# Two graph layers on one core: a head that shares the third pass's banks, moments on GpSimd, and a split weight load

## The chip, the cores and the metric

The kernel runs on one core of one Trainium2 chip. The metric is device time in microseconds (us) of one execution, lower being better; a kernel's time is the median of several executions. The engines are named as the profile names them: PE (matrix products), DVE (vector), ACT (scalar), POOL (GpSimd) and SP, which here only issues DMAs. PEld is PE's loading of stationary operands.

## The reference

Sixteen graphs of 1024 nodes with 128 channels go through two layers. Each layer ends in a residual sum and a normalisation over the channels. Cut to what matters:

```python
h = x                                              # layer 0: gated, 4 steps
for i in range(4):
    m = einsum('bjn,bjd->bnd', adj, h @ weight[i])
    gx, gh = m @ w_ih[i].T + b_ih[i], h @ w_hh[i].T + b_hh[i]
    r, z = sigmoid(xr + hr), sigmoid(xz + hz)      # thirds of gx and gh
    n = tanh(xn + r * hn)
    h = (1 - z) * n + z * h
x = layernorm(x + h * mask)

adj_d = dilate(adj)                                # layer 1: row by row, sequential
for k in 1, 2, 3:
    out = (adj_d @ h / deg) @ Wr[k] + h @ Wx[k] + b[k]
    h = h_k = bn(relu(out / norm(out) * mask))     # bn: moments over all graphs and nodes
x = layernorm(x + (concat(h_1, h_2, h_3) @ Wl + bl) * mask)
```

The batch norm of pass 3 takes its moments over all sixteen graphs, so the last product with `Wl` can't be finished for any graph before the third pass has ended for all.

## The kernel before, in words

**Layer 0** is the class `Gated` (`load_weights` L945, `prepare` L966, `load_test` L991, `layer` L1074, `run` L1131). Two streams of graphs alternate, a layer of one and then a layer of the other. A layer multiplies the state, split into two parts (`h_hi`, `h_lo`), with the adjacency matrix (PE, L1092), copies the product (ACT, L1095) and forms the gates from products with `h_wi` and `h_wh` (PE, L1104; DVE L1116 and L1118; ACT L1119; POOL L1123 to L1125). Before the first layer, `load_weights` loads for each of four steps one 128x128 matrix `h_w` and two gate matrices of 384x128 (`w_ih`, `w_hh`), and then two biases, all by ACT's DMA queue. `prepare` turns each of them on PE (L974 for the gates, L977 for `h_w`), evicts them (DVE and ACT, L975 and L978), and folds `h_w` into the first gate matrix (L981, L982). Adjacency (`h_a` L1016, `f_a` L687) and node data (`h_x` L1021) come by POOL's queue, which casts. For a check that the adjacency matrix is binary, `load_test` loads 32 blocks of 128x1024 `h_test` by SP's queue, the first at the start; DVE looks at each (`look`, L2028).

Beside layer 0 runs the dilation, class `FixPoint`: DVE scans (L737) and small operations, wide ACT passes `f_u`, DVE `f_nr` (L866), stores by SP (L867). The two are interleaved by hand: `beside` gives `layer` the work of the other stream and the next step of the dilation at numbered places. Nearly the whole kernel stands in manual schedules, where each engine executes its instructions in the order of the program text; only the stretches outside (`weights`, `head_weights`) are ordered by a planner, which may move an instruction ahead of its place.

**Layer 1** is the class `Sage`: three passes and a head. The **third pass** (`third`, L1875) takes 32 units, two halves of 512 nodes for each graph, in a software pipeline. In iteration i, PE forms the two products of unit i (`out_next`: L1800 into `q_oa`, L1803 and L1806 into `q_ob`) and turns the rows of unit i-3 (`turned`, L1450, into `s_tr`). DVE makes the reciprocal norms of unit i-2 (L1434 to L1436), and POOL scales its rows by them (`rows_by_pool`, L1439, four instructions, into `s_r`); then DVE takes the statistics of unit i-5 over its turned rows `s_r3` (L1909). ACT scales unit i (L1393, into `s_o`), DVE adds to it (L1396), ACT copies the turned rows of unit i-4 (L1916), ACT and DVE share the sums of squares (L1412, L1415, root L1419), and DVE adds the unit's share of the final product to `s_acc` (L1927). `s_o` and `s_r` have three buffers each, the PSUM tiles two. A flag for the binary check is read in iteration 16. Five iterations drain the pipeline; in these the rows are scaled by DVE (L1429).

`head_weights` (L1369) then forms the batch norm from all statistics, scales the last third of `Wl` by it, and makes the constant row `v` by four small products (L1377 and L1380), which `parts` cuts into three bf16 parts (L1343 and following).

The **head** (`last`, L1931) takes sixteen graphs. For each half PE forms four products of 128x128 with the kept rows (L1953), for the second half adds `s_acc` by a product with the unit matrix (L1957, 128x512), and adds the constant row by four short bf16 products with a node mask (L1961, its row `u_rb` from POOL, L1942). DVE adds `s_acc` in the first half (L1964). Then DVE takes statistics (L1968, eight of 128x128 for each graph) and aggregates them to mean and variance (L1970, eight of 128x2). ACT takes the root (L1972), DVE the reciprocal (L1977) and the shift (L1978). The eight blocks are normalised one graph later, one by POOL (L1984), seven by ACT (L1988), and stored by SP (L1990). The head has a pool of eight PSUM banks, two for each graph.

Of the kernel before, what the change touches and what calls it, by code (L numbers as in the profile page):

```python
# [917 lines left out]
class Gated:  # L918
# [28 lines left out]
    def load_weights(self):  # L947
# [262 lines left out]
class Sage:  # L1210
# [664 lines left out]
    def third(self):  # L1875

        nc, tc = self.nc, self.tc
        with ExitStack() as c:
            pool = lambda name, **k: c.enter_context(tc.tile_pool(name=name, **k))
            self.wk = pool("t_wk", bufs=3)  # L1880
            self.ps2 = pool("t_ps2", bufs=2, space=PSUM)
# [7 lines left out]
            for i in range(len(units) + 5):  # L1889
# [17 lines left out]
                if i >= 5:  # L1907
                    b3, f3 = units[i - 5]
                    nc.vector.bn_stats(self.stats[2][:, 2 * b3 + f3, :], self.r3[:, b3, f3, :])  # L1909
# [14 lines left out]
                if i < len(units):  # L1924
                    g["ss", f] = self.shared_squares(g["o", f])
                    acc = self.acc[:, b, 4 * f:4 * f + 4, :]
                    nc.vector.tensor_add(acc, pb[:, :, 1, :], acc)  # L1927


    def last(self, r48):  # L1930
        nc, tc, cst = self.nc, self.tc, self.cst  # L1931
        with ExitStack() as c:
            pool = lambda name, **k: c.enter_context(tc.tile_pool(name=name, **k))
            wk = pool("u_wk", bufs=6)
            ps = pool("u_ps", bufs=8, space=PSUM)
            c.enter_context(tc.manual_schedule(engines={ET.PE, ET.DVE, ET.Activation, ET.Pool, ET.SP}))
            st = {}

            def row(b):
# [4 lines left out]
            def head(b):  # L1944
                rb = st.pop(("row", b))
                row(b + 2)
                y = wk.tile([P, NB, C], F32, name="u_y")
                mv = self.small.tile([P, NB, 2], F32, name="p_mv")
                for f in range(2):
                    acc = self.acc[:, b, 4 * f:4 * f + 4, :]  # L1950
                    pp = ps.tile([P, 4, C], F32, name="u_p")
                    for i in range(4):
                        nc.tensor.matmul(pp[:, i, :], self.r3[:, b, f, i * P:(i + 1) * P], self.wr2,  # L1953
                                         start=(i == 0), stop=False)
                    if f:

                        nc.tensor.matmul(pp.rearrange("p a b -> p (a b)"), cst["ident"],  # L1957
                                         acc.rearrange("p a b -> p (a b)"), start=False, stop=False)
                    for i in range(4):
                        k = 4 * f + i  # L1960
                        nc.tensor.matmul(pp[:, i, :], self.mask48[:, k * P:(k + 1) * P], rb,  # L1961
# [155 lines left out]
```

## Time and profile before

| | |
|---|---|
| median of 3 runs | 2175.93 us (2174.55 to 2177.75) |
| the profiled execution | 2176.16 us |
| its span in the profile | 2174.3 us |
| mean TensorE clock granted | 0.988 of full |
| third pass, first L1800 to last statistics | 1985.86 to 2102.25 us |
| last product of the head ends | 2161.27 us |
| last store issued | 2166.43 us |

One execution was taken by the profiler, and its times are counted from the start of its span. A row of a timeline gives start, duration, engine, line, operation, tiles out<-in, shapes and how many instructions in one row; in square brackets stands how long the engine had been idle before it and what released it. In a table by stage each engine has its busy time and its instructions, followed by the granted clock, the DMA share and the GB/s. In a list of waits, the numbers are us in total, times, and the longest. Matmul ends are modelled. A wait for several events is put down to the one that came last by the profile.

### The profile page before, as it was taken

Reading aid. Unit: us, or ns where it says so; the run is one execution under the profiler, and the core shown is the slowest. Engines: PE = TensorE matmul, PEld = TensorE weight load, DVE = VectorE, ACT = ScalarE, POOL = GpSimd, SP = SyncE. Lnnn points to the kernel's source line nnn. Section 1 sums busy time; section 2 is a strip of 40 time slices with the busy share of each in tenths; the row PEclk is TensorE's granted clock in tenths of the full one; section 3 lists DMA queues with packets and bytes.
Section 4 is the critical chain, followed back from the end, with each engine's and each line's share of the span. In section 5 each row is a group of like instructions: output and inputs, shape, how many; then the busy total and the mean of one; then the engine's idle time right before and its main releaser. Section 6 shows DMA issues by size and latency. Waiting matters only on the chain. (4 is left out here: it accounts for less than half of the span.)

```text
span 2174.3 us, 33161 instructions
## 1 busy us (share of the span) xinstructions
PE 2063.3 (95%) x10217; PEld 1438.1 (66%) x10217; DVE 1831.1 (84%) x4313; ACT 1312.8 (60%) x3142; POOL 1324.3 (61%) x1346
## 2 busy tenths in 40 slices
PE   6999999999999999999999978999999889999987
PEld 3666556666556665566655656777777768887876
DVE  4898998988998889998889978888888777676888
ACT  3657557566565656656566466666666545555757
POOL 4458558567467476476575456777777545555852
PEclk9999999999999999999999989999999999999989
DMA  8348356347446276455394349888888677775515
GB/s 258 77 93 252 92 126 225 82 133 214 101 143 195 75 210 155 96 190 132 79 266 104 74 166 318 305 297 307 304 305 306 209 243 271 265 262 185 158 40 157
DMA packets 233856, 406.16 MB, mean 187 GB/s; under 512 B 79042, under 2 KB 100196, under 8 KB 233668
## 3 DMA queue, kind: packets, MB, share of 16 engines
q1 hardware_dynamic: 187844, 284.37, 40.7%
q0 software_dynamic: 41472, 117.46, 20.1%
q10 hardware_dynamic: 4352, 2.11, 0.4%
q8 instruction: 83, 1.36, 0.3%
q14 instruction: 105, 0.86, 0.1%
HBM read 313.48 MB, written 109.25 MB: 194 GB/s over the span
## 5 line engine op out<-in xcount | busy, mean ns | idle before, releaser
L1104 PE MATMUL h_g<-h_h,h_wh 128*128 128x512 f32 x768 | 396.1, 597 | 3.3 <-DVE h_r L1116 3.3
L1104 PE MATMUL h_g<-h_ms,h_wi 128*128 128x512 f32 x768 | 392.3, 592 | 0.0
L1123 POOL TENSOR_TENSOR h_zh<-h_r,h_h 128x512 f32<-128x512 f32 x126 | 174.1, 1382 | 257.9 <-ACT h_r L1119 254.7
L737 DVE TENSOR_TENSOR_SCAN f_rank<-f_a,f_first,f_pd 128x1024 f16<-128x1024 bf16 x128 | 299.4, 2345 | 4.2
L1092 PE MATMUL h_g<-h_a,h_hi 128*128 128x512 f32 x1024 | 278.6, 413 | 1.1 <-DMA h_a<-in_adj_dram 1.0
L1536 POOL CAST p_b<-p_at 128x512 uint8<-128x512 f32 x256 | 219.4, 878 | 84.3 <-DVE p_at L1528 52.3
L1104 PEld LDWEIGHTS h_g<-h_ms,h_wi 128*128 128x128 f32 x768 | 145.6, 190 | 184.2 <-issue 168.6
L1092 PE MATMUL h_g<-h_a,h_lo 128*128 128x512 f32 x1024 | 261.9, 393 | 0.4 <-DVE h_lo L1030 0.4
L1092 PEld LDWEIGHTS h_g<-h_a,h_hi 128*128 128x128 f32 x1024 | 190.1, 188 | 61.7 <-issue 21.0
L1092 PEld LDWEIGHTS h_g<-h_a,h_lo 128*128 128x128 f32 x1024 | 189.8, 188 | 39.0 <-DVE h_lo L1030 0.8
L1104 PEld LDWEIGHTS h_g<-h_h,h_wh 128*128 128x128 f32 x768 | 133.4, 190 | 100.3 <-issue 72.9
L1125 POOL TENSOR_TENSOR h_h<-h_h,h_zh 128x512 f32<-128x512 f32 x126 | 179.9, 1427 | 9.9
L1119 ACT ACTIVATE h_r<-h_r,h_bi 128x512 f32<-128x512 f32 x128 | 92.4, 722 | 150.1 <-DVE h_r L1118 150.1
L1124 POOL TENSOR_TENSOR h_zh<-h_z,h_zh 128x512 f32<-128x512 f32 x126 | 162.0, 1285 | 9.9
L1095 ACT COPY h_ms<-h_g 128x512 f32<-128x512 f32 x128 | 73.8, 576 | 150.7 <-PE h_g L1092 150.7
L1403 ACT ACTIVATE s_junk<-s_o 128x128 bf16<-128x128 f32 x256 | 76.1, 298 | 141.6 <-DVE s_o L1396 141.6
L910 ACT ACTIVATE f_u<-f_rank,f_q 128x128 f16<-128x128 f16 (+7 forms) x128 | 110.6, 867 | 69.7 <-DVE f_rank L850 69.7
L2028 DVE SCALAR_TENSOR_TENSOR p_junk<-p_a 128x1024 bf16<-128x1024 f32 x96 | 125.8, 1311 | 0.0
L1803 PE MATMUL q_ob<-s_wxp,q_xt 128*128 128x256 f32 x512 | 123.5, 385 | 0.0
L778 POOL TENSOR_SCALAR_AFFINE_SELECT f_both<-f_both 128x512 bf16<-128x512 bf16 x32 | 20.4, 639 | 164.2 <-DVE f_both L777 164.2
L1528 DVE SCALAR_TENSOR_TENSOR p_at<-p_nr,p_u 128x128 fp32r<-128x128 bf16 (+1 forms) x192 | 102.4, 543 | 20.2 <-ACT p_at L1520 14.8
L887 ACT ACTIVATE f_pd<-f_rank,f_q 128x128 f32<-128x128 f16 x128 | 59.1, 462 | 96.6 <-DVE f_q L701 93.4
(273 smaller groups left out, 4900.9 us busy)
## 6 DMA issues: line engine op xcount, KB each, us to landing
h_a<-in_adj_dram POOLq DMA_DIRECT2D x128, 512.0 KB, 9.1
p_a<-in_adj_dram SPq DMA_DIRECT2D x96, 512.0 KB
f_a<-in_adj_dram POOLq DMA_DIRECT2D x128, 256.0 KB, 6.5
e_nr<-f_nr SPq DMA_DIRECT2D x128, 256.0 KB
p_nr<-e_nr SPq DMA_DIRECT2D x32, 1024.0 KB
h_test<-in_adj_dram SPq DMA_DIRECT2D x32, 512.0 KB
s_at<-p_b SPq DMA_DIRECT2D x32, 512.0 KB
s_ag<-s_ag SPq DMA_DIRECT2D x64, 256.0 KB
```

The lines of the kernel that those rows point to most:

```text
L737: nc.vector.tensor_tensor_scan(out, a, other[:, 0, 0:1].to_broadcast([P, N]), start, op0=ALU.add, op1=ALU.bypass)
L910: nc.scalar.activation(u[:, :n1], rank[:, g, :n1], AF.Abs, bias=q[:, 1, g:g + 1], scale=q[:, 0, g:g + 1])
L1092: nc.tensor.matmul(pm[f], part[:, j, :], st.adj[j][:, half[f]], start=(j == 0 and n == 0), stop=(j == NB - 1 and n == 1))
L1104: nc.tensor.matmul(pg, lhs, rhs, start=(i == 0), stop=(i == len(mm) - 1))
L1119: nc.scalar.activation(r, r, AF.Tanh, bias=bias(self.bi, 2))
L1123: aid.tensor_tensor(d, r, h, ALU.subtract)
L1124: aid.tensor_tensor(d, z, d, ALU.mult)
L1125: aid.tensor_tensor(h, h, d, ALU.add)
L1528: self.nc.vector.scalar_tensor_tensor(g["at"][:, j, c0:c0 + low], v[:, j, c0:c0 + low], 0.0, pu[:, :low], op0=ALU.is_lt, op1=ALU.is_lt)
L1536: self.nc.gpsimd.tensor_copy(g["b", f][:, j, :], g["at"][:, j, f * HF:(f + 1) * HF].bitcast(F32))
L1803: nc.tensor.matmul(pb[:, i], g["xt"][:, f, blk], self.wxp, start=(i % 2 == 0), stop=False)
L2028: nc.vector.scalar_tensor_tensor(junk, a, 0.0, a, op0=ALU.is_gt, op1=ALU.not_equal, accum_out=bad[:, c:c + 1])
```

## The change

1. Of the weights of layer 0, the four matrices `w_hh` and both biases are loaded by SP's queue; `h_w` and `w_ih` stay on ACT's.
2. The first `h_test` is loaded by POOL's queue; it stands where the program text has it, after the first layer's work on that queue. The other 31 stay on SP's.
3. In the third pass the statistics (L1909 before) are taken of unit i-4 and stand at the end of the iteration, behind L1927; before they were of unit i-5 and stood behind L1436. The drain has four iterations in place of five. The last L1927 is put off into `head_weights`.
4. Third pass and head share one PSUM pool (`q_oa`, `q_ob`, `s_tr`, two buffers each, eight banks in all), and `head_weights` stands inside the head's manual schedule. A graph whose number leaves 1 or 2 when divided by 4 takes one two-bank tile `q_ob`; the others take two tiles of one bank.
5. In the drain and between the weight products stand the unit-matrix products of the first three graphs (`start_half`) and eight bf16 products of 128x512 whose result nobody reads.
6. In the head, `half` (products with the kept rows) runs two halves ahead of `finish` (the constant row and the statistics).
7. For all graphs but the last, mean and variance come from six POOL instructions on 128x8 (`moments`) in place of eight L1970 on DVE; the factors that this leaves out go into ACT's root and DVE's shift. The last graph keeps the eight L1970.
8. POOL normalises two blocks of each graph in place of one, ACT six in place of seven. The root of graph b follows the normalisation of graph b-1 on ACT. `u_rb` has four buffers in place of three, and DVE makes the first.

```diff
-                nc.scalar.dma_start(t, src[l].rearrange("(g p) c -> p g c", p=C))
+                (nc.scalar, nc.sync)[n].dma_start(t, src[l].rearrange("(g p) c -> p g c", p=C))
         for t, src in zip(self.b_in, (b_ih, b_hh)):
-            nc.scalar.dma_start(t, src.rearrange("l (g c) -> (l g) c", c=C))
+            nc.sync.dma_start(t, src.rearrange("l (g c) -> (l g) c", c=C))
...
-            self.nc.sync.dma_start(self.test, self.adj[n // 2, n % 2 * P:(n % 2 + 1) * P, :])
+            (self.nc.sync if n else self.nc.gpsimd).dma_start(self.test, self.adj[n // 2, n % 2 * P:(n % 2 + 1) * P, :])
...
-    def head_weights(self, ps):
+    def head_weights(self):
         nc, K = self.nc, 3 * B
+        v = self.ps2.tile([P, 4, P], F32, name="s_tr")[:K, 0, :]
+        junk = self.ps2.tile([P, 4, P], F32, name="s_tr").rearrange("p a b -> p (a b)")
         self.batch_norm(2)
         self.scaled(self.wr2, self.wl[:, 2, :], 2)
-        v = ps.tile([K, C], F32, name="s_v48")
         for l in range(3):
             beta = self.small.tile([C, K], F32, name="s_beta48")
             nc.vector.tensor_copy(beta, self.ab[l][:, 1:2].to_broadcast([C, K]))
+            if l == 2:
+                self.start_half(1)
+                for i in range(8):
+                    nc.tensor.matmul(junk, self.cst["ident_b"], self.mask48[:, :HF], start=True, stop=True)
             nc.tensor.matmul(v, beta, self.wl[:, l, :], start=(l == 0), stop=False)
         beta = self.small.tile([C, K], F32, name="s_beta48")
         nc.vector.tensor_copy(beta[:10, :], self.cst["ident"][:10, 9:10].to_broadcast([10, K]))
         nc.tensor.matmul(v, beta[:10, :], self.vr, start=False, stop=True)
+        nc.vector.tensor_add(*self.late)
+        self.start_half(2)
         r48 = self.one.tile([P, C], BF, name="s_r48")
         nc.gpsimd.memset(r48, 0.0)
         self.parts(v, self.part48, r48[:K, :])
         return r48
+
+    def head_banks(self, b):
+        ps = self.ps2
+        if b % 4 in (0, 3):
+            self.banks[b] = [ps.tile([P, 4, C], F32, name="s_tr" if b % 4 else "q_oa") for f in range(2)]
+        else:
+            t = ps.tile([P, 4, 2, C], F32, name="q_ob").rearrange("p a b c -> p (a b) c")
+            self.banks[b] = [t[:, :4, :], t[:, 4:, :]]
+
+    def start_half(self, b):
+
+        acc = self.acc[:, b, 4:, :]
+        self.head_banks(b)
+        self.nc.tensor.matmul(self.banks[b][1].rearrange("p a b -> p (a b)"), self.cst["ident"],
+                              acc.rearrange("p a b -> p (a b)"), start=True, stop=False)
...
-            self.ps2 = pool("t_ps2", bufs=2, space=PSUM)
+            self.banks = {}
...
-            for i in range(len(units) + 5):
+            for i in range(len(units) + 4):
...
+                if i == len(units):
+                    self.start_half(0)
                 if 2 <= i < len(units) + 2:
                     b1, f1 = units[i - 2]
                     g = self.g[b1]
                     rows = self.rows_by_pool if i < len(units) else self.rows
                     g["r", f1] = rows(b1, f1, g.pop(("o", f1)), g.pop(("ss", f1)))
-                if i >= 5:
-                    b3, f3 = units[i - 5]
-                    nc.vector.bn_stats(self.stats[2][:, 2 * b3 + f3, :], self.r3[:, b3, f3, :])
...
-                    nc.vector.tensor_add(acc, pb[:, :, 1, :], acc)
-
-
-    def last(self, r48):
+                    self.late = acc, pb[:, :, 1, :], acc
+                    if i + 1 < len(units):
+                        nc.vector.tensor_add(*self.late)
+                if i >= 4:
+                    b4, f4 = units[i - 4]
+                    nc.vector.bn_stats(self.stats[2][:, 2 * b4 + f4, :], self.r3[:, b4, f4, :])
...
+    def last(self):
         nc, tc, cst = self.nc, self.tc, self.cst
         with ExitStack() as c:
             pool = lambda name, **k: c.enter_context(tc.tile_pool(name=name, **k))
             wk = pool("u_wk", bufs=6)
-            ps = pool("u_ps", bufs=8, space=PSUM)
             c.enter_context(tc.manual_schedule(engines={ET.PE, ET.DVE, ET.Activation, ET.Pool, ET.SP}))
+            r48 = self.head_weights()
             st = {}
             def row(b):
                 if b < B:
-                    st["row", b] = wk.tile([P, C], BF, name="u_rb", bufs=3)
-                    nc.gpsimd.tensor_scalar(st["row", b], r48, self.graph[:, b:b + 1], None, op0=ALU.mult)
...
+                    st["row", b] = wk.tile([P, C], BF, name="u_rb", bufs=4)
+                    (nc.gpsimd if b else nc.vector).tensor_scalar(st["row", b], r48, self.graph[:, b:b + 1], None,
+                                                                  op0=ALU.mult)
+            def half(b, f):
+                ahead = b < 3 and f
+                if f == 0:
+                    row(b + 2)
+                    if b not in self.banks:
+                        self.head_banks(b)
+                pp, acc = self.banks[b][f], self.acc[:, b, 4 * f:4 * f + 4, :]
+                for i in range(4):
+                    nc.tensor.matmul(pp[:, i, :], self.r3[:, b, f, i * P:(i + 1) * P], self.wr2,
+                                     start=(i == 0 and not ahead), stop=False)
+                if f and not ahead:
+                    nc.tensor.matmul(pp.rearrange("p a b -> p (a b)"), cst["ident"],
+                                     acc.rearrange("p a b -> p (a b)"), start=False, stop=False)
+            def finish(b, f):
+                pp, acc = self.banks[b][f], self.acc[:, b, 4 * f:4 * f + 4, :]
+                for i in range(4):
+                    k = 4 * f + i
+                    nc.tensor.matmul(pp[:, i, :], self.mask48[:, k * P:(k + 1) * P], st["row", b],
+                                     start=False, stop=(i == 3))
+                if not f:
+                    st["y", b] = wk.tile([P, NB, C], F32, name="u_y")
+                    st["s6", b] = self.small.tile([P, NB, 6], F32, name="u_st")
+                    nc.vector.tensor_add(st["y", b][:, :4, :], pp, acc)
+                s6, src = st["s6", b], pp if f else st["y", b]
+                for i in range(4):
+                    nc.vector.bn_stats(s6[:, 4 * f + i, :], src[:, i, :])
+            def moments(b):
+                y, pp, s6 = st.pop(("y", b)), self.banks.pop(b)[1], st.pop(("s6", b))
+                st.pop(("row", b))
+                if b < B - 1:
+                    mv = self.small.tile([P, 4, NB], F32, name="u_mv")
+                    total, gap, spread, var = (mv[:, i, :] for i in range(4))
+                    nc.gpsimd.tensor_tensor(gap, s6[:, :, 1], s6[:, :, 4], ALU.subtract)
+                    nc.gpsimd.tensor_tensor(spread, s6[:, :, 2], s6[:, :, 5], ALU.add)
+                    nc.gpsimd.tensor_tensor(gap, gap, gap, ALU.mult)
+                    nc.gpsimd.tensor_scalar(gap, gap, C / 4.0, 0.0, op0=ALU.mult, op1=ALU.add)
+                    nc.gpsimd.tensor_tensor(var, gap, spread, ALU.add)
+                    nc.gpsimd.tensor_tensor(total, s6[:, :, 1], s6[:, :, 4], ALU.add)
+                    st[b] = y, pp, total, var, -0.5, 1.0 / C
+                else:
+                    mv = self.small.tile([P, NB, 2], F32, name="p_mv")
+                    for k in range(NB):
+                        nc.vector.bn_aggr(mv[:, k, :], s6[:, k, :])
+                    st[b] = y, pp, mv[:, :, 0], mv[:, :, 1], -1.0, 1.0
+            def root(b):
+                rs = st["rs", b] = self.small.tile([P, 2, NB], F32, name="u_rs")
+                nc.scalar.activation(rs[:, 0, :], st[b][3], AF.Sqrt, bias=self.eps, scale=st[b][5])
             def norm(b):
...
+                y, pp, mean, _, share, _ = st.pop(b)
+                rs = st.pop(("rs", b))
                 nc.vector.reciprocal(rs[:, 0, :], rs[:, 0, :])
-                nc.vector.scalar_tensor_tensor(rs[:, 1, :], mv[:, :, 0], -1.0, rs[:, 0, :],
+                nc.vector.scalar_tensor_tensor(rs[:, 1, :], mean, share, rs[:, 0, :],
                                                op0=ALU.mult, op1=ALU.mult)
                 for k in range(NB):
                     src = pp[:, k - 4, :] if k > 3 else y[:, k, :]
                     scale, shift = rs[:, 0, k:k + 1], rs[:, 1, k:k + 1]
-                    if k == 0 or (b, k) == (B - 1, 1):
+                    if k < 2:
                         nc.gpsimd.tensor_scalar(y[:, k, :], src, scale, shift, op0=ALU.mult, op1=ALU.add)
                     elif b == B - 1 and k > 2:
                         nc.vector.tensor_scalar(y[:, k, :], src, scale, shift, op0=ALU.mult, op1=ALU.add)
...
             row(0)
             row(1)
...
+            halves = [(b, f) for b in range(B) for f in range(2)]
+            for h in range(len(halves) + 2):
+                if h < len(halves):
+                    half(*halves[h])
+                if h < 2:
+                    continue
+                b, f = halves[h - 2]
+                finish(b, f)
+                if f:
+                    moments(b)
+                    if b == B - 1:
+                        root(b)
+                    if b:
+                        norm(b - 1)
+                    if b < B - 1:
+                        root(b)
+            norm(B - 1)
...
-        self.third()
-        with tc.tile_pool(name="s_psw", bufs=1, space=PSUM) as ps:
-            r48 = self.head_weights(ps)
-        self.last(r48)
+        with tc.tile_pool(name="t_ps2", bufs=2, space=PSUM) as self.ps2:
+            self.third()
+            self.last()
```

More of the change, by code (lines that the diff above doesn't have):

```diff
@@ L1940, in row @@
                 if b < B:
-                    st["row", b] = wk.tile([P, C], BF, name="u_rb", bufs=3)
-                    nc.gpsimd.tensor_scalar(st["row", b], r48, self.graph[:, b:b + 1], None, op0=ALU.mult)
[L1944 to L1961, printed above, removed]
-                                         start=False, stop=(i == 3))
-                    if not f:
-                        nc.vector.tensor_add(y[:, :4, :], pp, acc)
-                    s6 = self.small.tile([P, 4, 6], F32, name="p_st")
-                    src = pp if f else y
-                    for i in range(4):
-                        nc.vector.bn_stats(s6[:, i, :], src[:, i, :])
-                    for i in range(4):
-                        nc.vector.bn_aggr(mv[:, 4 * f + i, :], s6[:, i, :])
-                rs = self.small.tile([P, 2, NB], F32, name="u_rs")
-                nc.scalar.activation(rs[:, 0, :], mv[:, :, 1], AF.Sqrt, bias=self.eps)
-                st[b] = y, pp, mv, rs
@@ L1975, in norm @@
+            def root(b):
+                rs = st["rs", b] = self.small.tile([P, 2, NB], F32, name="u_rs")
+                nc.scalar.activation(rs[:, 0, :], st[b][3], AF.Sqrt, bias=self.eps, scale=st[b][5])
             def norm(b):
-                y, pp, mv, rs = st.pop(b)
+                y, pp, mean, _, share, _ = st.pop(b)
+                rs = st.pop(("rs", b))
                 nc.vector.reciprocal(rs[:, 0, :], rs[:, 0, :])
-                nc.vector.scalar_tensor_tensor(rs[:, 1, :], mv[:, :, 0], -1.0, rs[:, 0, :],
+                nc.vector.scalar_tensor_tensor(rs[:, 1, :], mean, share, rs[:, 0, :],
@@ L1996, in last @@
             row(1)
-            for b in range(B + 1):
-                if b < B:
-                    head(b)
-                if b:
-                    norm(b - 1)
+            halves = [(b, f) for b in range(B) for f in range(2)]
[15 more added lines that the diff above has]
+            norm(B - 1)
     def run(self):
```

## The prediction

> **What bounds the kernel now.** I read the page first, then the waits of the first 45 us, then a table of busy time by stage, then the timelines of the third pass and of the head.
>
> ```profile
> span 2174.3 us, 33161 instructions
> PE 2063.3 (95%) x10217; PEld 1438.1 (66%) x10217; DVE 1831.1 (84%) x4313; ACT 1312.8 (60%) x3142; POOL 1324.3 (61%) x1346
> ```
>
> PE is the bound on average, but the change touches the three places where it is not, or shares the bound. In the start PE waits for weights:
>
> ```profile
> ACT L1056 <- DMA h_z<-in_L_gnn_w_ih_dram: 23.5, 1, 23.5
> PE h_g L974 <- DMA h_r<-in_L_gnn_w_ih_dram: 5.4, 1, 5.4
> PE h_g L974 <- DMA h_z<-in_L_gnn_w_ih_dram: 4.8, 1, 4.8
> PE h_g L974 <- DMA h_r<-in_L_gnn_w_hh_dram: 3.5, 1, 3.5
> PE h_g L974 <- DMA h_z<-in_L_gnn_w_hh_dram: 2.7, 1, 2.7
> ```
>
> ACT's first work comes at 23.5 because its queue is blocked by its own issues (6.54, 4.21 and 4.28 us at three of them). The last weights are turned at 28.02 and the first L1092 starts at 33.81.
>
> In the third pass one loop runs through three engines:
>
> ```profile
> 2072.88 0.68 DVE L1927 TENSOR_TENSOR s_acc<-q_ob,s_acc 128x512 f32<-128x512 f32 x1
> ...
> 2073.48 0.16 DVE L1434 TENSOR_SCALAR s_ss<-s_ss 128x4 f32<-128x4 f32 x1
> ...
> 2073.88 0.17 DVE L1436 TENSOR_TENSOR s_ss<-s_ss,mask 128x4 f32<-128x4 f32 x1
> 2073.97 0.69 DVE L1909 BATCH_NORM_STATS2 s_st<-s_r 128x6 f32<-128x512 f32 x1
> ...
> 2074.24 5.88 POOL L1439 TENSOR_SCALAR s_r<-s_o,s_ss 128x128 f32<-128x128 f32 x8 [0.79 <-PE s_tr L1450]
> ...
> 2077.16 1.14 ACT L1393 ACTIVATE s_o<-q_oa,s_rdeg 128x128 f32<-128x128 f32 x4 [0.70 <-POOL s_r L1439]
> ...
> 2078.39 0.69 DVE L1396 TENSOR_TENSOR s_o<-q_ob,s_o 128x512 f32<-128x512 f32 x1 [0.75 <-ACT s_o L1393]
> ```
>
> Read it as a ring: L1434 to L1436 end at 2074.05, POOL starts 0.19 later, ACT waits for POOL's fourth row, DVE waits for ACT, and L1927 ends where the next L1434 starts. The page names PE as POOL's releaser, but in three successive pairs POOL starts 0.19, 0.19 and 0.18 after L1436 ends and 0.50, 0.60 and 0.69 after L1450 starts: the constant one is the cause. A pair of units takes 6.69; PE needs 3.29 a unit (6.58 a pair), so ring and PE are nearly level.
>
> ```profile
> 2094.00:2107.00 13.00, 5.63 (x23) 2.96 (x22) 10.67 (x33) 4.62 (x15) 2.89 (x4) 0.71 0.00 1
> 2107.00:2114.00 7.00, 6.81 (x33) 5.32 (x34) 3.41 (x17) 0.00 (x0) 2.18 (x4) 0.57 0.00 0
> 2120.00:2156.00 36.00, 36.00 (x297) 29.59 (x297) 35.25 (x215) 32.24 (x91) 11.21 (x22) 1.00 0.58 162
> ```
>
> In the drain PE idles 7.4 us and works at half clock until 2113.0; in the head it is busy 36.00 of 36 (3.20 us a graph), with DVE at 35.25.
>
> ```profile
> 2142.27 0.89 DVE L1968 BATCH_NORM_STATS2 p_st<-u_p 128x6 f32<-128x128 f32 x4
> ...
> 2143.55 0.17 DVE L1978 SCALAR_TENSOR_TENSOR u_rs<-p_mv,u_rs 128x8 f32<-128x8 f32 x1
> ...
> 2143.76 1.26 ACT L1988 ACTIVATE u_y<-u_y,u_rs 128x128 f32<-128x128 f32 x3
> ...
> 2144.92 1.48 ACT L1988 ACTIVATE u_y<-u_p,u_rs 128x128 f32<-128x128 f32 x4
> ```
>
> **What the Trainium skill says.** "DMA: Bandwidth & Descriptors", Queues, rings and completion order: a DMA engine alternates between its queue rows packet by packet. Agrees: from 6 to 26 us POOL's queue moves about 84 packets a us (2 or 4 KB, 173 ns) and ACT's about 89 (512 B, 39 ns). "TensorE: Matmul & The Clock Gate", Part 1: the clock halves after an idle window and needs some 3.4 us of work to return; Part 4: transposes do not count as work. Agrees: last product 2094.1, half clock at 2099.7 though L1450 ran, full at 2113.0. "SBUF — State Buffer", Who interferes with whom: a DVE instruction with one SBUF input does not block GpSimd. So moving L1909 should leave POOL's row at 733 ns; no trace here isolates it. "GPSIMD Engine Reference", 3.1: some 2.6 cycles an element for two inputs, which for 8 elements is under 20 ns as an estimate, so fixed cost rules the new small operations; none is in this trace.
>
> **Part by part.**
>
> 1. *Half the gated weights by SP.* 1536 of 3584 packets leave ACT's row. With three rows a turn takes 173+39+39 = 251 ns instead of 212, so each small row moves 89 x 212/251 = 75 a us. h_test's 128 packets of 4 KB also leave the first 5 us: 128 x 173/16 = 1.4 us in which, at the 540 a us that 512 B packets reach alone, some 750 weights move. At 6 us 739 had landed; now about 1500. Of the other 2084 half per row: 1042/75 = 13.9, so the last lands near 20 by rate, and I take 21.7 (20.5 to 23.5) for the issues that still block each other. Behind it 5.8 us as before: L1092 at 27.5, **-6.3** (-4 to -8.3). SP pays six issues of some 0.5 us and any wait in them; its next instruction (L867) comes at 61.03, so that costs nothing, and if that cover were gone, 3.
>
> 2. *First h_test by POOL's queue.* Issued behind the first layer's L1125, which ended 58.8; POOL's loads of 512 KB took from 3.0 to 5 us to land, I take 3.5: 62.3. (The issue itself takes 0.57 of POOL, ahead of L1123, which waits for ACT 254.7 us in all; without that cover it would cost 0.57.) DVE's look, at 57.83 and in order, waits 4.5; the look itself took 2.04 against 1.29 usually (0.75 back), and DVE idled 1.35 in the next 7 us. Behind it are f_nr, L1116, L1118 and L1030, whose end releases PE's L1104 (68.82). 4.5 - 0.75 - 1.35 = **+2.4** (1 to 4). What is late next is L867's store and the turned copy behind it (61.03), by the same 2 to 3.
>
> 3. *L1909 moved behind L1927.* It filled the time in which DVE awaits ACT (0.75); now it stands between L1927 and L1434, in the ring: 6.69 + 0.67 = 7.36 a pair, 3.68 a unit for 3.34. About 24 units run so (of 32; the first few fill the buffers and the last two are turned by DVE): 24 x 0.34 = 8.2; the stall at the flag (2019 to 2024) takes up to 1.8: **+7.5** (5 to 9.5). Below zero is excluded: nothing leaves the ring. The drain's iteration less is in the next item.
>
> 4. *Drain and weights of the head.* Before, two of the three weight products ran ahead of the moments (PE 2101.57). Now all follow program order: two more copies on DVE, the L1957-like product of 0.86 warm or 1.71 cold, eight idle products of 0.21 or 0.43, then two last products. v is ready at 2108.5 warm, 2110.9 cold, against 2106.1. But the three unit products (0.86 each) are then mostly done, and PE runs on without pauses: 0.86 + 32x0.95 + 13x0.86 + 32x0.22 = 49.5, to 2160.1 if cold to 2109.7, or 2157.6 warm, against 2161.27. After the last product DVE has the eight L1970 and three blocks of statistics: 7.2 to the last store against 5.1. I take cold, since the pause that cools the clock comes before the first of these products: -1.2 + 2.1 = **+1.0** (-1.5 to +2.5). The late add (0.60) lies beside the idle products.
>
> 5. *Moments by GpSimd.* Eight L1970 (0.60) leave DVE per graph; what hides that is PE, whose products of a graph (0.95, 0.86, 0.22, 0.95, 0.22) fill 3.20 anyway: nothing. POOL: two rows of 0.44, u_rb 0.60, six small operations: nearest 182 ns (48x3 select) and 106 (memset), I take 0.2: 2.7 of 3.20. Cover gone at 0.29 each. ACT's root follows with 0.3 to spare.
>
> 6. *Shared banks, halves two ahead.* The bank of graph b+4 is wanted when PE ends graph b+2, 6.4 after b; before, at 9.6. It is free when ACT has normalised b: graph b+1's end (3.2) + statistics 1.01 + L1977, L1978 0.41 + 2x0.39 + 1.48 = 3.7, with semaphores 3.8: 7.0. Where a graph has one two-bank tile (remainders 1 and 2 of b by 4) PE waits 0.6, once in four graphs as the next is then late already: 3 x 0.6 = **+1.8** (0 to 2.4).
>
> Sum: -6.3 + 2.4 + 7.5 + 1.0 + 1.8 = +6.4. The profiled execution took 2176.16 (span 2174.3 and 1.9 around): 2182.6. The median is 0.23 lower: **2182.3**.
>
> **Rivals.** (a) *Faster:* L1909 is free, because POOL really waits for PE's L1450 as the page says and 0.67 fits the ring's slack; it decides from a slack of 0.67 a pair. Third 0, clock kept warm -1.5, no bank wait: 2176.2 - 3.9 - 1.5 = 2170.8, median 2170.6. For: ring and PE differ by only 0.11 a pair. Against: the constant 0.19. (b) *Nearly same:* the ring costs 5, no bank wait, start -4.5: 2176.2 + 0.5 + 1 = 2177.7. (c) *POOL bound in the head:* at 0.4 each its graph takes 3.9: 14 x 0.7 = 9.8 in place of 1.8: 2190.3. (d) *DVE's relief counts:* 15 x 0.6 = -9 on the sum: 2173.3; against it PE's 36.00 of 36.
>
> **How the numbers follow.** Forecast 0.51 (own range 2179 to 2186), (a) 0.14, (b) 0.24, (c) 0.07, (d) 0.04. A measurement tells 0.2% (4.35 us) from no change. Slower: 0.48 of the forecast and (c), 0.55; same: (b), the forecast's rest and part of (d), 0.30; faster: (a) and a rest, 0.15. The range of 2174 to 2188 leaves out (a) and most of (c).
>
> **What would show it.** L1800 starting every 3.68 with L1909 between L1927 and L1434; L1092 at 27.5; a DVE wait of 4.5 at h_test; PE waits of 0.6 at graphs 5, 9 and 13; half clock until v. Wrong if L1800 keeps 3.34, if POOL fills its graph, or if weights land after 26.

## The result and the profile after

The changed kernel takes 2181.24 us (median of 18 runs, 2178.84 to 2186.63), the kernel before 2175.87 (18 runs). The ratio is 1.0024 (95% interval 1.0018 to 1.0030): slower by 5.4 us, against 6.4 forecast. The profiled execution has a span of 2181.1 us, 6.8 more than before.

```profile
span 2181.1 us, 33176 instructions
PE 2070.4 (95%) x10224; PEld 1440.3 (66%) x10225; DVE 1826.2 (84%) x4194; ACT 1306.9 (60%) x3127; POOL 1348.7 (62%) x1451
```

The shares have hardly moved, though DVE lost 119 instructions and POOL gained 105: these lines say nothing about this change. The stages do. Rows left out are marked by dots. First the waits of the first 45 us:

```profile
ACT L1056 <- DMA h_w<-in_L_gnn_weight_dram: 6.4, 1, 6.4
...
PE h_g L974 <- DMA h_z<-in_L_gnn_w_ih_dram: 4.9, 1, 4.9
PE h_g L974 <- DMA h_zh<-in_L_gnn_w_ih_dram: 4.2, 1, 4.2
...
PE h_g L974 <- DMA h_r<-in_L_gnn_w_ih_dram: 2.6, 1, 2.6
```

ACT is free at 6.4 instead of 23.5, PE no longer waits for the second gate matrices, and the first L1092 starts at 29.02 instead of 33.81. The packets of each queue from 9 to 15 us (q0 is POOL's queue, q1 SP's, q10 ACT's), the change first, then the kernel before:

```profile
q0 software_dynamic: 508, 0.97, 80.5%
q1 hardware_dynamic: 490, 0.24, 19.1%
q10 hardware_dynamic: 510, 0.24, 14.3%
```

```profile
q0 software_dynamic: 564, 1.21, 90.4%
q10 hardware_dynamic: 563, 0.27, 22.2%
```

Split over two queues, the weights moved 1000 packets in this time instead of 563. From 50 to 80 us, the price of the late `h_test`:

```profile
DVE h_junk L2089 <- DMA h_test<-in_adj_dram: 4.6, 1, 4.6
...
PE h_g L1104 <- DVE h_r L1116: 0.5, 1, 0.5
```

DVE waits 4.6 us, but PE is idle for only 0.5 of it. Then the third pass, near the stretch that was shown before (L1439 is now L1461, L1909 is L1953, L1927 is L1950, L1800 is L1822):

```profile
2076.93 0.69 DVE L1950 TENSOR_TENSOR s_acc<-q_ob,s_acc 128x512 f32<-128x512 f32 x1
...
2077.53 0.69 DVE L1953 BATCH_NORM_STATS2 s_st<-s_r 128x6 f32<-128x512 f32 x1
...
2078.23 1.14 ACT L1415 ACTIVATE s_o<-q_oa,s_rdeg 128x128 f32<-128x128 f32 x4 [0.70 <-POOL s_r L1461]
...
2078.41 1.06 PE L1822 MATMUL q_oa<-s_wr,q_agi 128*128 128x128 f32 x8
...
2078.89 2.98 POOL L1461 TENSOR_SCALAR s_r<-s_o,s_ss 128x128 f32<-128x128 f32 x4 [0.70 <-ACT s_o L1415]
...
2079.45 0.69 DVE L1418 TENSOR_TENSOR s_o<-q_ob,s_o 128x512 f32<-128x512 f32 x1 [0.76 <-ACT s_o L1415]
...
2082.09 1.06 PE L1822 MATMUL q_oa<-s_wr,q_agi 128*128 128x128 f32 x8
```

The statistics stand between L1950 and the reciprocal norms that POOL needs, and L1822 starts every 3.68 us. In the kernel before, PE kept its own pace of 3.29, with the ring close behind it (ACT's last twelve scales came every 3.34):

```profile
2074.09 1.06 PE L1800 MATMUL q_oa<-s_wr,q_agi 128*128 128x128 f32 x8
...
2077.38 1.06 PE L1800 MATMUL q_oa<-s_wr,q_agi 128*128 128x128 f32 x8
```

The profile names ACT as POOL's releaser, before it named PE. The distances point to DVE: the statistics give way to the next instruction at 2078.13, three small instructions take 0.57, and POOL starts 0.19 later at 2078.89, the same 0.19 as before. From ACT's last copy ahead of the pass (L1623, before L1601) to the end of the last statistics it is 126.9 us, before 118.7.

The drain, on PE (L1382 and L1385 are the weight products, L1405 the unit products, L1381 the idle ones):

```profile
2108.16 1.06 PE L1382 MATMUL s_tr<-s_wl,s_beta 128*48 128x128 f32 x4 [3.95 <-DVE s_beta L1377]
2109.15 2.08 PE L1405 MATMUL q_ob<-s_acc,ident 128*128 128x512 f32 x2
2111.01 0.63 PE L1381 MATMUL s_tr<-s_mask,ident_b 128*128 128x512 bf16 x1
...
2113.55 0.42 PE L1382 MATMUL s_tr<-s_wl,s_beta 128*48 128x128 f32 x2
```

In the kernel before, two of the three weight products ran ahead of the moments:

```profile
2101.57 1.09 PE L1377 MATMUL s_v<-s_wl,s_beta 128*48 128x128 f32 x4 [0.67 <-ACT s_r L1916]
2104.82 0.66 PE L1377 MATMUL s_v<-s_wl,s_beta 128*48 128x128 f32 x2 [2.17 <-DVE s_beta L1376]
```

Now PE idles 3.95 us before the first product, where before it idled 2.17 before the third, and the constant row can be read 8.8 us after the last statistics (2105.55 to 2114.35), before 3.9. Half clock lasted 13.65 us in both profiles. In the head:

```profile
2128.80 1.16 PE L1980 MATMUL q_ob<-s_wr,s_r 128*128 128x128 f32 x8 [0.62 <-ACT u_y L2038]
...
2142.28 1.16 PE L1980 MATMUL q_ob<-s_wr,s_r 128*128 128x128 f32 x8 [0.46 <-ACT u_y L2038]
...
2155.75 1.16 PE L1980 MATMUL q_ob<-s_wr,s_r 128*128 128x128 f32 x8 [0.46 <-ACT u_y L2038]
```

These are the bank waits at graphs 5, 9 and 13, 1.54 us in all. From unit product to unit product these three graphs take 4.04, 3.87 and 3.87 us and the others 3.20, as before, so each wait costs a little more than its idle time, 2.2 together. From the end of PE's last product (2166.02) to the last SP store (2172.94) it is 6.9 us, before 5.0.

### The profile page after: what moved, and what is told of

It is laid out like the page before. It is cut to its first block, busy times and chain, and to the rows that moved or that the text cites. A ratio compares the mean times of both kernels' runs of the same rounds, so it can differ in the third digit from the quotient of the medians.

```text
span 2181.1 us, 33176 instructions
## 1 busy us (share of the span) xinstructions
PE 2070.4 (95%) x10224; PEld 1440.3 (66%) x10225; DVE 1826.2 (84%) x4194; ACT 1306.9 (60%) x3127; POOL 1348.7 (62%) x1451
## 5 line engine op out<-in xcount | busy, mean ns | idle before, releaser
L1104 PE MATMUL h_g<-h_h,h_wh 128*128 128x512 f32 x768 | 396.1, 597 | 3.8 <-DVE h_r L1116 3.8
L1104 PE MATMUL h_g<-h_ms,h_wi 128*128 128x512 f32 x768 | 392.2, 592 | 0.0
L1092 PE MATMUL h_g<-h_a,h_hi 128*128 128x512 f32 x1024 | 278.4, 413 | 0.5 <-DMA h_a<-in_adj_dram 0.3
L1104 PEld LDWEIGHTS h_g<-h_ms,h_wi 128*128 128x128 f32 x768 | 145.5, 190 | 184.3 <-issue 168.2
L1092 PE MATMUL h_g<-h_a,h_lo 128*128 128x512 f32 x1024 | 262.2, 393 | 0.1
L1092 PEld LDWEIGHTS h_g<-h_a,h_hi 128*128 128x128 f32 x1024 | 190.1, 188 | 60.9 <-issue 21.5
L1092 PEld LDWEIGHTS h_g<-h_a,h_lo 128*128 128x128 f32 x1024 | 189.6, 188 | 39.2 <-DVE h_lo L1030 1.1
L1104 PEld LDWEIGHTS h_g<-h_h,h_wh 128*128 128x128 f32 x768 | 133.3, 190 | 101.1 <-issue 72.6
L1119 ACT ACTIVATE h_r<-h_r,h_bi 128x512 f32<-128x512 f32 x128 | 92.4, 722 | 151.8 <-DVE h_r L1118 151.8
```

The source lines that it names most:

```text
L1092: nc.tensor.matmul(pm[f], part[:, j, :], st.adj[j][:, half[f]], start=(j == 0 and n == 0), stop=(j == NB - 1 and n == 1))
L1104: nc.tensor.matmul(pg, lhs, rhs, start=(i == 0), stop=(i == len(mm) - 1))
L1119: nc.scalar.activation(r, r, AF.Tanh, bias=bias(self.bi, 2))
```

## The experiments

The bare number is each run's median; the kernel before, run beside them, had 2175.5 to 2175.9. "As changed" means the changed kernel with only the edit shown.

**Statistics back in their old place.**

```diff
-            for i in range(len(units) + 4):
+            for i in range(len(units) + 5):
...
                     g["r", f1] = rows(b1, f1, g.pop(("o", f1)), g.pop(("ss", f1)))
+                if i >= 5:
+                    b3, f3 = units[i - 5]
+                    nc.vector.bn_stats(self.stats[2][:, 2 * b3 + f3, :], self.r3[:, b3, f3, :])
...
-                if i >= 4:
-                    b4, f4 = units[i - 4]
-                    nc.vector.bn_stats(self.stats[2][:, 2 * b4 + f4, :], self.r3[:, b4, f4, :])
```

> Only the statistics of the third pass go back to their old place (of unit i-5, behind the reciprocal norms, five drain iterations); all else as changed. Ring theory (statistics lengthen the ring of reciprocal norms, GpSimd rows, ACT scale and DVE adds by 0.67 us a pair): L1822 starts every 3.34 us again instead of 3.68, the last statistics end 8 us earlier less about 0.5 for the longer drain, time 2173 to 2174 us against 2181 of the changed kernel. Rival (the third pass is longer through the shared banks or the put-off add): spacing stays 3.68 and the time stays at 2181.

2172.35, ratio 0.9986 (0.9978 to 0.9993). The pass takes 118.7 us again, and L1822 is back near PE's pace:

```profile
2073.68 1.06 PE L1822 MATMUL q_oa<-s_wr,q_agi 128*128 128x128 f32 x8
2077.09 1.06 PE L1822 MATMUL q_oa<-s_wr,q_agi 128*128 128x128 f32 x8
```

The place of the statistics is worth more than the whole loss: with them in their old place the change is faster than the kernel before.

**Four buffers of s_o.**

```diff
-        o = self.wk.tile([P, 4, C], F32, name="s_o")
+        o = self.wk.tile([P, 4, C], F32, name="s_o", bufs=4 if scalar else None)
```

> The changed kernel with four buffers of s_o in the third pass in place of three; nothing else. Ring theory: ACT's scale of unit i then waits for GpSimd's rows of unit i-4, the ring is open, and PE's own 3.29 us a unit decides: last statistics 9 to 12 us earlier than in the changed kernel, time 2170 to 2172 us, although the statistics stand where the change put them. Rival (DVE's program order alone makes 3.68, the buffer has no part): spacing stays 3.68, time 2181. Rival 2 (PE's turned rows release GpSimd): 3.34 at most, no better than before.

2171.05, ratio 0.9977 (0.9968 to 0.9986), with the statistics where the change put them. From 2030 to 2080 us ACT waits for POOL once (as changed, 14 times from 2040 to 2090), and PE sets the pace:

```profile
2066.78 1.06 PE L1822 MATMUL q_oa<-s_wr,q_agi 128*128 128x128 f32 x8
...
2068.29 1.12 ACT L1415 ACTIVATE s_o<-q_oa,s_rdeg 128x128 f32<-128x128 f32 x4
2068.40 0.68 DVE L1953 BATCH_NORM_STATS2 s_st<-s_r 128x6 f32<-128x512 f32 x1
...
2070.07 1.06 PE L1822 MATMUL q_oa<-s_wr,q_agi 128*128 128x128 f32 x8
```

3.29 us a unit, 114.6 for the pass. So it was a ring, engines that wait for one another in a circle, closed by there being only three buffers; DVE's order alone doesn't make 3.68. (This execution also had an early first L1092, 26.06, which is no part of the edit.)

**The blocks in PSUM first.**

```diff
-                for k in range(NB):
+                for k in (0, 1, 4, 5, 6, 7, 2, 3):
```

> The changed kernel, but ACT normalises the four blocks that lie in PSUM (k 4 to 7) before those in SBUF (k 2 and 3). Bank theory: the two-bank tile comes free 2 x 0.39 = 0.77 us earlier, so the three waits of 0.62, 0.46 and 0.46 us of PE at graphs 5, 9 and 13 go and the head is 1.5 us shorter: 2179.7. Rival (PE waits for ACT's last block or for the output buffer): the waits stay, 2181.

2179.60, ratio 1.0017 (1.0011 to 1.0024). The interval overlaps that of the change as made; the trace is clearer: no PE wait for ACT is left in the head, no graph from the third on takes more than 3.34 us, and from the last statistics to the last store it is 65.4 us, as changed 67.4. The waits were for the bank.

**Moments by DVE for all graphs.**

```diff
-                if b < B - 1:
+                if b < 0:
```

> The changed kernel, but all sixteen graphs take mean and variance by eight aggregating instructions of DVE, as the last graph does; GpSimd keeps only its rows and two blocks. Theory (PE bounds the head at 3.20 us a graph and DVE's relief is worth nothing by itself): the period stays 3.20 to 3.25, but the 0.6 us of DVE before the reciprocal lengthens each of the three bank waits, +1 to +3 us: 2182 to 2184. Rival (DVE's relief is what holds the head at 3.20): 0.6 us for each of 15 graphs, +9 us: 2190. Rival 2 (GpSimd's moments are the bound): faster, below 2180.

2183.82, ratio 1.0038 (1.0024 to 1.0052), which overlaps that of the change as made. In the trace the same three waits grew:

```profile
PE q_ob L1980 <- ACT u_y L2038: 2.6, 3, 0.9
```

1.5 us became 2.6, and the tail 0.7 longer; between the waits the period is still 3.20. DVE's relief of 0.6 us a graph is worth nothing for the period, but a little where ACT's normalisation holds a bank.

**Without the idle products.**

```diff
-                for i in range(8):
+                for i in range(0):
```

> The changed kernel without the eight idle products (their result is read by nobody). In the changed kernel's profile PE works without a pause from 2108.2, the clock is back at about 2112, and the idle products lie from 2111.0 to 2113.5 ahead of the third weight product. Theory A (PE would be busy anyway with the unit product before and the unit and row products after, so the clock returns as early, and the idle products only stand in the way): the constant row comes 2.4 us earlier, time 2178.8. Theory B (they keep the clock up): without them the half clock lasts some 3 us longer, which costs the head products 1.5 us and more: 2180 to 2183.

2181.02, ratio 1.0025 (1.0017 to 1.0032): no difference from the change as made, and both theories have half of it. The constant row came 1.9 us sooner after the statistics (6.9), but the clock came back later, although PE worked without a pause:

```profile
2110.00:2112.00 2.00, 2.00 (x6) 0.95 (x5) 1.02 (x4) 0.00 (x0) 0.00 (x0) 0.50 0.00 0
2112.00:2114.00 2.00, 2.00 (x8) 1.48 (x8) 1.37 (x6) 0.00 (x0) 0.45 (x1) 0.50 0.00 0
2114.00:2116.00 2.00, 2.00 (x19) 2.00 (x19) 0.00 (x0) 0.00 (x0) 1.32 (x3) 0.94 0.00 0
```

The clock (the third number from the end) returns at 2114.24, 7.6 us after PE became busy at 2106.6. As changed it took 4.3, and in five other profiles that have the idle products 4.3 to 5.8. The length of the stretch is no measure of this: it is 17.07 here and 13.65 as changed, but 6.83 in three other runs with the same drain (those of the PSUM order, the moments by DVE and `h_test` by SP), where it began later. The idle products seem to bring the clock back sooner, and cost what they bring; the kernel without them was profiled once.

**The first h_test by SP.**

```diff
-            (self.nc.sync if n else self.nc.gpsimd).dma_start(self.test, self.adj[n // 2, n % 2 * P:(n % 2 + 1) * P, :])
+            self.nc.sync.dma_start(self.test, self.adj[n // 2, n % 2 * P:(n % 2 + 1) * P, :])
```

> The changed kernel with the first h_test on SP's queue, behind the gate matrices and biases, in place of GpSimd's. DVE's wait of 4.6 us is gone. Theory A (as the prediction had it: the wait costs 2.4 us): 2179 to 2179.5. Theory B (PE lost only 0.47 us by it, the rest lay in DVE's slack, and the 128 packets of 4 KB now share the queues with the last weights, 0 to 1.4 us): 2180.8 to 2182.

2182.57, ratio 1.0028 (1.0017 to 1.0039). The DVE wait is gone, and nothing is gained. The time alone can't decide, as the first L1092 starts at 30.00: in this run and the next, with `h_test` on SP's queue, it starts at 30.00 and 30.27, with the split and `h_test` on POOL's queue at 25.90 to 29.11 in nine profiles. The 128 packets of `h_test` seem to cost the start something, as theory B has it. The traces decide on theory A, the prediction's step. Take as lead the distance by which PE starts the same L1104 sooner than in the kernel before. At 68 us, behind the late look, it drops from 4.78 to 4.04 in the change, and by 0.7 to 1.0 in all seven profiles with the late `h_test`; in this run and three others with it in time it doesn't move. The wait costs PE less than half of the 2.4 that theory A needs.

**The split of the weight load alone, in the kernel before.** The edits are the two of `load_weights`.

> The kernel before with only the split of the weight load: the four second gate matrices and the biases by SP's queue; h_test stays on SP's queue and so comes behind them. Theory: the first L1092 at 29 to 30.5 in place of 33.8, and the gain is kept to the end as it is in the changed kernel (4.8 at the first product, 4.8 at the third pass): 2171 to 2172.5. Rival (the gain is given back, as the dilation or the adjacency loads decide later): 2175 to 2176.

2172.66, ratio 0.9985 (0.9979 to 0.9992). The first L1092 starts at 30.27, 3.5 us early, ACT's first and last L1119 of layer 0 are 3.5 and 3.3 us early, and the third pass begins 3.0 early: most of the gain at the start is kept.

**Four buffers of s_o in the kernel before.** The edit is that of the second run.

> The kernel before with four buffers of s_o in the third pass in place of three. Ring theory: the ring of 6.69 us a pair held it back too, only a little behind PE: L1800 starts every 3.29 throughout, the pass is 1.5 to 3.5 us shorter, 2172.5 to 2174.5. Rival (PE is the bound of the third pass before, the ring only rides on it): no change, 2175.6.

2172.86, ratio 0.9987 (0.9979 to 0.9995): the three buffers held the kernel before too, by 2.9 us. But not in the steady part of the pass, where L1800 starts every 3.29 in both. In the profiles the pass is 2.5 shorter: 0.8 behind the last L1800, and 1.7 at the product for the flag, which needs a buffer of `s_tr` that ACT, itself held by POOL, has not yet copied out. In the kernel before:

```profile
2022.68 1.14 ACT L1393 ACTIVATE s_o<-q_oa,s_rdeg 128x128 f32<-128x128 f32 x4 [0.54 <-POOL s_r L1439]
...
2023.70 0.60 ACT L1916 COPY s_r<-s_tr 128x512 f32<-128x512 f32 x1
...
2024.36 0.19 PE L1921 MATMUL s_tr<-l_col,l_max 128*1 128x1 f32 x2 [1.32 <-ACT s_r L1916]
```

The last four runs are of use for their times only. They share an edit in layer 0 that leaves out the turning of blocks in the dilation's read-back, so that what is read back is not what the dilation needs; the dilation's own comparison of its result then never counts:

```diff
-            self.nc.sync.dma_start(rt[:, old], self.not_r[b0 + g, old, k * P:k * P + P], transpose=True)
+            self.nc.sync.dma_start(rt[:, old].rearrange("p (a c) -> p a c", c=P),
+                                   self.not_r[b0 + g, old, k * P:k * P + P].rearrange("(a p) c -> p a c", p=P))
...
-            self.nc.sync.dma_start(self.left[i + 1, g][:, cols], nr[:, k * P:k * P + P], transpose=True)
+            self.nc.sync.dma_start(self.left[i + 1, g][:, cols], nr[:, k * P:k * P + P])
...
-            fix.nc.vector.scalar_tensor_tensor(junk, again, 1.0, self.x, op0=ALU.mult, op1=ALU.not_equal,
+            fix.nc.vector.scalar_tensor_tensor(junk, again, 0.0, self.x, op0=ALU.mult, op1=ALU.is_gt,
```

> Base for the three that follow: the kernel before, with the DMA that turns blocks of the dilation's result replaced by plain copies of the same blocks (so the turning of these blocks is left out, and the dilation's last check compares so that it never counts). All else is as before. Theory (SP's transposing copies lie beside other work): within 4 us of 2175.7, third pass and head as in the kernel before to 0.1 us. Rival (they hold the dilation): some us faster or slower in layer 0 only.

2177.94, ratio 1.0007 (0.9998 to 1.0015): this base is not told apart from the kernel before, though its median is 2.5 us higher and its profile begins the third pass 5.2 us later. The last three are therefore compared by their stages.

**Early products and a short lead.**

```diff
-        self.batch_norm(2)
-        self.scaled(self.wr2, self.wl[:, 2, :], 2)
         for l in range(3):
+            if l == 2:
+                self.batch_norm(2)
+                self.scaled(self.wr2, self.wl[:, 2, :], 2)
...
-                b, f = halves[h - 2]
-                finish(b, f)
+                while todo and len(halves) - len(todo) <= h - (2 if h < 17 else 0):
+                    b, f = todo.pop(0)
+                    finish(b, f)
```

> The changed kernel (the same plain copies in the dilation, turning left out), with two mendings that touch different stages. First, the first two products of the head's weights and their copies stand ahead of the batch norm, with the unit product of graph 1 and the idle products. Second, the halves run two ahead only up to graph 8; then each is finished at once. Program-order theory: from the last statistics to the constant row in place of 8.8 us some 4 (3.9 before), head products 4.5 earlier. Rival: the idle time is at half clock and gives under 2. Tail theory: from the last product to the last store 4.7 in place of 6.7, since the last three halves no longer reach DVE together. Rival: the eight aggregations alone make it, 6.5. From the last statistics to the last store 60.2 if both theories hold, against 66.9 in the changed kernel and 63.7 before.

2180.52, ratio 1.0023 (1.0016 to 1.0031). Both stages went as the theories had it, and yet little is gained. The constant row is ready 3.3 us after the last statistics, the head products start 4.2 after them (as changed 9.7), the tail is 4.7 us. But the short lead has a wait of its own:

```profile
2136.45 2.02 PE L1982 MATMUL q_ob<-s_wr,s_r 128*128 128x128 f32 x8 [3.15 <-DVE u_y L1997]
...
2142.34 1.16 PE L1982 MATMUL q_ob<-s_wr,s_r 128*128 128x128 f32 x8 [0.82 <-DVE u_y L1997]
```

There are four such waits, 5.6 us in all, at the second halves of graphs 9, 10, 13 and 14 and at no other graph behind the eighth. In these four both halves lie in one tile, and by the profile the write to its second bank is made to wait for DVE's reading of the first. With two halves in advance PE has written before DVE is asked to read. Behind the wait of 3.15 the clock was at half for 3.4 us. From the last statistics to the last store it is 66.6 us, as changed 67.4, and not 60.7 (60.2 was expected to an event 0.5 sooner). Neither mending was measured by itself.

**All mendings, with the head of the change and with the head before.** The first adds four s_o, the PSUM order and an early `h_test` (called behind the second stream's `load_adj`) to the run above; the second takes the split, the early `h_test`, four s_o and the statistics' new place into the kernel before.

> The changed kernel (plain copies in the dilation) with all mendings: four buffers of s_o, PSUM blocks normalised first, short lead, early products, the first h_test by GpSimd's queue directly behind the second stream's adjacency. If the costs found one by one add up: 2171 (four s_o) less 0.5 (h_test) less 1.5 (waits) less 1.9 (tail) less 4.5 (early products) = 2162.6, plus what the base of this series differs from the kernel before. If they overlap: 2165 to 2168.

> The kernel before (plain copies in the dilation) with what was found good outside the head: gate matrices and biases split between the queues, the first h_test by GpSimd's queue behind the second stream's adjacency, four buffers of s_o, statistics of unit i-4 behind the last addition with four drain iterations; its head as before. Start -6 (first L1092 at 28.0 as the mean of the profiles, against 34.3), third pass -4: 2165.5 plus what the base differs. If h_test delays the adjacency or the gains overlap: 2168 to 2170. Against the mended head of the change it tells what the head's redesign is worth: 63.7 from the last statistics to the last store here.

2168.79, ratio 0.9966 (0.9954 to 0.9978), and 2166.99, ratio 0.9964 (0.9950 to 0.9978). Both beat the kernel before by some 7 us or more, and the changed one by 12 or more; they are not told apart from each other. The first missed its sum by 6.2, the second by 1.5. In the first, most of the miss lies in the head: the waits of the short lead are there again (5.8 us), and from the last statistics to the last store it takes 66.0, the head before 63.1. So the new head, as far as it was tried, is the slower one; with early products and the long lead it wasn't tried.

## Why the prediction was right, step by step

The cause of the loss was right, the statistics in the ring. One step failed, the late `h_test`, and in this pair of profiles it was covered by another miss: the start gained 1.5 less than forecast, and `h_test` cost about 2 less. That these two cancel is luck.

1. *Split load, -6.3.* The mechanism held: from 9 to 15 us each of the two small queues moved some 80 packets a us, where 75 was forecast. This profile gives -4.8, but the start varies from execution to execution: seven profiles with this start have their first L1092 at 26.06 to 29.11 (mean 27.7), three with the old start at 33.8, 34.7 and 34.8. The mean gain is 6.7, as forecast. The profiled execution of the change is 1.9 us above the median of its runs, and its late start accounts for 1.3 of that; so the spans differ by 6.8 and the medians by 5.4.
2. *Late h_test, +2.4.* This step failed. "DVE's look waits 4.5" was right (4.6), but the sum took the wait, less two small credits, as PE's loss. PE lost 0.74 (0.7 to 1.0 in seven profiles), and by the third pass the lead over the kernel before was 4.8 again: drifts of this size in layer 0 hide the term. The wait should have been followed to PE's next real dependence.
3. *Statistics in the ring, +7.5.* 8.1 in this pair. Over the profiles the pass takes 117.0 to 118.7 us with the old order and three buffers (four profiles), 124.8 to 126.9 with the new (six): 8.3 between the means. Two edits show the cause, one at the statistics and one at the buffer. The stall at the flag gave back nothing of the 1.8 that was allowed for it: L1822 stood 5.28 and 5.07 us apart there, L1800 before 5.10 and 3.56. A stretch of 3.41 us at half clock fell into it, worth 1.0 (without it, in two other runs, the second distance is 4.1); the profile before had such a stretch in the pass's first unit, worth 1.7, which hides a like part. POOL's rows took 746 ns each, before 733: the moved statistics hardly touch them.
4. *Drain and weights, +1.0.* From the last statistics to PE's end +1.3, of which 2.2 are the bank waits, so -0.9 in place of -1.2; the tail +1.9 in place of +2.1: together +1.0. Cold was the right choice: half clock lasted through the unit products of the first two graphs. One reading was off: the product that ends at 2094.1 is L1450's, the one before it ends at 2093.7, and half clock came at 2099.4. That the turning doesn't count as work isn't shown by it, since PE was idle for most of that time.
5. *Moments by GpSimd, 0.* The six small instructions take 199 to 209 ns, 0.2 was taken. The period stays 3.20. That it shortens the bank waits by 1.1 us was not foreseen.
6. *Bank waits, +1.8.* Three, at the graphs named, idle for 1.54 and worth 2.2; without them the head is 2.0 shorter.

What was measured in this pair of profiles up to the last store: -4.8 for the start, 0 for `h_test`, +8.1, +1.0 and +2.2, together +6.5; another 0.3 lies behind it, and the span is longer by 6.8. With the means over profiles for the first three terms, -6.7 + 0.9 + 8.3 + 1.0 + 2.2 = +5.7, beside 5.4 between the medians.

Rival (a) fell with the first two runs: the ring has no slack of 0.67. So did rival (b), which gave the ring 5 and no bank wait. Rival (c) fell with the 0.2 us of POOL's small operations, rival (d) with the fourth run.

## What to carry to other kernels

Before moving an instruction within an in-order loop, find the ring that sets the pace and see whether the new place lies on it: here an instruction of 0.67 us, moved within the loop body, cost 8 us, and one more buffer took the ring apart wherever it stood. The releaser that a profile names is a guess; an event whose distance to the start is constant is the better candidate, and an edit at it is the test. A wait on an engine that is not the bound costs only what the bound's next dependence on it feels: 4.6 us of DVE were 0.7 to 1.0 of PE.

## What the runs showed of the hardware

- Half clock came in multiples of 3.41 us (3.41, 6.83, 13.65, 17.07). In the drain it ended 4.3 to 5.8 us after PE became busy in six profiles with idle bf16 products among its work, and 7.6 us after in the one with float32 products alone. In the short lead a PE wait of 3.15 us was followed by a stretch of 3.41. So was a stretch of 3.41 us in which PE was busy for 1.94 (1983.37 to 1986.78 in the kernel before): PE did not stand still in it.
- Two queues that load weights in small packets moved 1000 packets in 6 us beside POOL's 508, one queue 563 beside POOL's 564: the queues came out nearly equal in packets, not in bytes.
- The same start differed by 3 us between executions (first L1092 at 26.06 to 29.11), and the landing of the last weights with it: in the profile with the start at 26.06 the last packet of the weights started at 19.4, in the change's own at 21.8.
- The six small GpSimd instructions on 128x8 float32 take 199 to 209 ns each, the normalisation of a block of 128x128 448: sixteen times the elements in 2.2 times the time.
